# Branch prefetch hints and the order of first loads in a four-layer graph network on one core

## The chip, the cores and the metric

The kernel runs on one core of a Trainium2 chip. The metric is device time in microseconds (us); lower is better. The engines are TensorE (PE, with its weight loads as PEld), VectorE (DVE), ScalarE (ACT), GpSimd (POOL) and SyncE (SP), which only issues DMA transfers. An engine's sequencer is written with a q (DVEq): it takes instructions in order, waits on semaphores, branches and issues transfers.

## The reference

Four graph layers run one after another on 4096 nodes with 256 features, each followed by a residual sum and a layer norm. Only layers 0 and 2 meet the change.

```python
# layer 0: attention over all nodes, 8 heads of 32 channels
node_feats = (x @ W.T + b).reshape(4096, 8, 32)
logits = leaky_relu(parent[:, None, :] + child[None, :, :], 0.2)
logits = where(abs(adj) != 0, logits, 0)
out = einsum('ijh,jhc->ihc', softmax(logits, axis=1), node_feats)
...
# layer 2: two steps of diffusion R @ Xf and of top-p attention A @ Xa
for n in range(2):
    A = top_p_attention(Xa, W1, W2, W3)
    Xf, Xa = R @ Xf, A @ Xa
    Z = Z + Xf @ U1[n].T + Xa @ U2[n].T
```

## The kernel before

**Layer 0** has two stages. In the first (`sums0`, L421) the adjacency is read once. PE forms, for every node, sums over its neighbours (L601); DVE turns them into the tensor `zd` in DRAM, 33 numbers per node and head (32 channels and a count; L568 to L574). The same pass writes the adjacency as bytes (`nad`) and factored features (`gmd`) to DRAM. The engines' order in this loop is written out by hand (`manual_schedule`), over slots n of four column blocks each.

A flag `fits` says whether the factored way is safe for these numbers. If it is 0, `choose0` (L375) runs `general0`, a slow general way. For these inputs the flag is 1: every engine loads it (TENSOR_LOAD), takes the branch over `general0` (COMPARE_BRANCH) and goes on behind it. At the join each engine brings its semaphores to the value that the skipped code would have left (EVENT_SEMAPHORE on L375); SP does so for the semaphores of the transfers, which includes a wait for the last stores of `zd`.

In the second stage (L298 to L370) there are two halves of four heads; each half goes over four blocks `it` of 1024 rows, and each block over its four heads `hh`. One head is 8 groups g of four column blocks, and per group 32 matmuls (L331, 256 per head) of a mask `gt` with `gm`, the factored features. ACT or DVE compare the row logits `lpb` (a broadcast row of 512 KB) with column logits (`sg`, L270 and L276), and DVE ands the result with the bytes `na` (L272, L278) to form `gt`, of which there are four buffers. When a head's matmuls are done, DVE reduces `acc` (L337), scales it, adds the head's part of `zd` (tile `z`, L345) and divides.

The first head of all has its first two groups prepared in the first stage (`gt0`, `gm0`, `first`), so PE can start on them at once; its loads begin with group 2 and wrap round. The order of DMA issues before the change:

- SP: per group `na` (L301, 512 KB) and the first head's `gm` (L303, 198 KB); then the other heads' `gm` (L306, 396 KB for two groups)
- POOL: per head `lpb` (L236) and `z` (L316, 1024 pieces of 132 bytes), two buffers each
- ACT and POOL: the weights of layers 1 and 2 that `add_w1` (L778) loads: w1 (256 KB) and its bias on ACT, three attention weights (144 KB) on POOL

In this stage a scheduler sets the order of each engine's instructions, and may move a load ahead of others when it is ready: `add_w1` stands at the end of the layer in the code, and its loads are issued at 579 to 585 us.

**Layer 2** runs two steps over 32 row blocks, again in a hand-written order (`manual_schedule`), eight sections s per block. After the last but one block a flag `row` says whether any row needs mending; `mend` (L1270) holds the code for that, and it is branched over here, once per step. The last block's products follow behind the branch: transposes (L1405, L1498), their products (L1414), and diffusion products (L1617) whose pieces SP loads (L1603).

Of the kernel before, what the change touches and what calls it, by code (L numbers as in the profile page):

```python
# [9 lines left out]
F32 = mybir.dt.float32  # L10
# [9 lines left out]
ET = mybir.EngineType  # L20
# [3 lines left out]
P = 128  # L24
# [26 lines left out]
def row_broadcast(v, n):  # L51

    return bass.AP(tensor=v.tensor, offset=v.offset, ap=[[0, P], [1, n]])


class Net:
# [159 lines left out]
    def layer0(self):  # L216
        nc, tc, NB, D, N = self.nc, self.tc, self.NB, self.D, self.N
        H, C = 8, 32
# [5 lines left out]
        with ExitStack() as ctx:  # L224
# [7 lines left out]
            fac = pool.tile([P, 4, NB, H], F32, name="fac")  # L232
            lpd = dram.tile([H, N], F32, name="lpd")

            def row_logits(t, h, it):
                nc.gpsimd.dma_start(t, bass.AP(tensor=lpd.tensor, offset=lpd.offset + h * N + it * IT, ap=[[0, P], [1, IT]]))  # L236
                return t

            first = pool.tile([P, IT], F32, name="lpb0")
# [51 lines left out]
            gm = gp.tile([P, NB, H // 2, 6 * C1], BF16, name="gm")  # L291
            na = gp.tile([P, NB, IT], U8, name="na")

            later = []
            per_head = Q // 2 // (H // 2)
            for half in range(2):
                for it in range(N // IT):
                    i0 = it * Q  # L298
                    begun = 2 if it == half == 0 else 0
                    for g in [*range(begun, NB // K), *range(begun)]:  # L300
                        nc.sync.dma_start(na[:, g * K:(g + 1) * K], nad[it, :, g * K:(g + 1) * K, :])  # L301
                        if it == 0:
                            nc.sync.dma_start(gm[:, g * K:(g + 1) * K, 0], gmd[half, :, g * K:(g + 1) * K, 0])  # L303
                    for hh in range(1, H // 2 if it == 0 else 0):
                        for g in range(0, NB // K, 2):
                            nc.sync.dma_start(gm[:, g * K:(g + 2) * K, hh], gmd[half, :, g * K:(g + 2) * K, hh])  # L306
                    if half:
                        nc.sync.dma_start(X[:, i0:i0 + Q, :], xr[:, i0:i0 + Q, :])
                        y0 = work.tile([P, Q, D // 2], F32, name="y0", bufs=1)
                        nc.sync.dma_start(y0, yd[i0:i0 + Q].rearrange("b p d -> p b d"))  # L310
                    y = work.tile([P, Q, H // 2, C], F32, name="y")
                    for hh in range(H // 2):
                        h = half * (H // 2) + hh
                        lpb = row_logits(work.tile([P, IT], F32, name="lpb"), h, it) if h or it else first
                        z = work.tile([P, Q, C1], F32, name="z")
                        nc.gpsimd.dma_start(z, zd[i0:i0 + Q, :, h].rearrange("b p c -> p b c"))  # L316
                        acc = psum.tile([P, Q, 256], F32, name="acc")
                        for g in range(NB // K):

                            head0 = g < 2 and half == it == hh == 0  # L320
                            if head0:
                                gt = gt0[:, g * K:(g + 1) * K, :]
                            else:
                                gt = work.tile([P, K, IT], FP8, name="gt", bufs=4)
                                sg = work.tile([P, K, IT], FP8, name="sg", bufs=3)
                                mask(gt, sg, na[:, g * K:(g + 1) * K, :], lpb, g, h)
                            for k in range(K):
                                jc = g * K + k
                                for q in range(Q):

                                    nc.tensor.matmul(acc[:, q, :6 * C1], gt[:, k, q * P:(q + 1) * P],  # L331
                                                     gm0[:, jc, :] if head0 else gm[:, jc, hh, :],
                                                     start=(jc == 0 and q % 2 == 0),
                                                     stop=(jc == NB - 1 and q % 2 == 1))

                        red = work.tile([P, Q, 2 * C1], F32, name="red")
                        nc.vector.tensor_reduce(red, acc[:, :, :6 * C1].rearrange("p q (s c) -> p q c s", s=3),  # L337
                                                AX.X, ALU.add)

                        red = red.rearrange("p q (s c) -> p q s c", s=2)  # L340
                        nc.vector.tensor_mul(red, red, fac[:, 0:2, i0:i0 + Q, h].rearrange("p s q -> p q s").unsqueeze(3)
                                             .to_broadcast([P, Q, 2, C1]))
                        t1 = red[:, :, 0, :]
                        nc.vector.tensor_add(t1, t1, red[:, :, 1, :])
                        nc.vector.tensor_add(t1, t1, z)  # L345
                        r = work.tile([P, Q], F32, name="r")
                        nc.vector.reciprocal(r, t1[:, :, C])
                        nc.vector.tensor_mul(y[:, :, hh, :], t1[:, :, :C], r.unsqueeze(2).to_broadcast([P, Q, C]))
                        for xs in later[:per_head]:
                            self.layernorm(work, xs, xs, nc.gpsimd, bufs=6)  # L350
                        del later[:per_head]
                    y = y.rearrange("p q h c -> p q (h c)")
                    if not half:
                        nc.gpsimd.dma_start(yd[i0:i0 + Q].rearrange("b p d -> p b d"), y)
                        continue

                    if i0 + Q == NB:
                        self.add_w1()
                    engine = nc.vector if i0 + Q == NB else nc.gpsimd
                    for q in range(0, Q, 2):  # L360
                        xs = X[:, i0 + q:i0 + q + 2, :]
                        nc.gpsimd.tensor_add(xs[:, :, :D // 2], xs[:, :, :D // 2], y0[:, q:q + 2])
                        engine.tensor_add(xs[:, :, D // 2:], xs[:, :, D // 2:], y[:, q:q + 2])
                        later.append(xs)
# [7 lines left out]

    def choose0(self, fac, zd, gmd, gm0):

        with self.tc.If(self.nc.values_load(self.fits, min_val=0, max_val=1) == 0):  # L375
            self.general0(fac, zd, gmd, gm0)

    def factors0(self, wp, work, ps, both, nlc, fac):
# [42 lines left out]
    def sums0(self, both, nlc, fac, lpd, nad, zd, gmd, then, early_mask):  # L421
# [6 lines left out]
        with ExitStack() as ctx:  # L428
# [147 lines left out]
            with tc.manual_schedule(engines={ET.PE, ET.Activation, ET.DVE, ET.Pool, ET.SP}):  # L576
# [4 lines left out]
                for b in range(0, NB, 2):  # L581
                    pz = [psz.tile([P, 2, 512], F32, name="pz") for _ in range(2)]
                    masks = early_mask(work, (b - NB + 12) // 2) if NB - 12 <= b < NB - 4 else iter(())
                    for g in range(groups):
                        n = b // 2 * groups + g
                        load(n + 2)
                        cast(n + 1)
                        if g % 4 == 0:
                            stages = factored(b + g // 4)
                        if before and g < 2:  # L590
                            closed(b - 2, g, before[g])
                        next(stages)
                        if g in (3, 5):
                            next(masks, None)
                        ar = ready.pop(n)
                        for q in range(2):
                            for k in range(G):
                                jc = g * G + k
                                for s in range(2):
                                    for t in range(2):  # L600
                                        nc.tensor.matmul(pz[q][:, t, :W], ar[:, q, k, :], src[:, jc, t, s],  # L601
                                                         start=(jc == 0 and s == 0), stop=(jc == NB - 1 and s == 1))
                    before = pz
# [173 lines left out]

    def add_w1(self):  # L778
        nc, pool = self.nc, self.pool1
        self.weight1, self.bias1 = self.load_w(pool, self.w1, "w1"), self.load_row(pool, self.b1, "bias1")  # L780
        aw1, aw3, aw2, _ = self.attention_parts()
        for t, w in ((aw1, self.aw1t), (aw3, self.aw3t)):
            nc.gpsimd.dma_start(t, w.rearrange("(c p) m -> p c m", p=P))
        nc.gpsimd.dma_start(aw2, self.aw2t)

    def attention_parts(self):

# [78 lines left out]
    def layer2(self):  # L866
# [3 lines left out]
        with ExitStack() as ctx:  # L870
# [395 lines left out]
            def mend(step, row, flag, e, r, made=()):  # L1266


                spare = es[(NB - 2) % 3][:, :N]
                with tc.If(flag == 0):  # L1270
                    for i in range(N // 512):
                        nc.sync.dma_start(kT[:, i * 512:(i + 1) * 512].bitcast(F32), kd[i])
                    with tc.For_i(0, NB - 1, 1) as b:
# [372 lines left out]
            for step in range(2):  # L1646
# [62 lines left out]
                with tc.manual_schedule(engines=five):  # L1709
                    for b in range(NB - 1):  # L1710
# [14 lines left out]
                        for s in range(8):  # L1725
# [63 lines left out]
                                nc.sync.dma_start(kd[b - 2], kT[:, cols].bitcast(F32))  # L1789
                            if s == 0 and difs:  # L1790
                                whole(difs)
                            if s == 4 and not ahead:
                                row = settled()
                                next(row)
# [260 lines left out]
```

## Time and profile before

| what | us |
|---|---|
| median of 3 runs (3929.32 to 3931.58) | 3931.0 |
| the profiled execution | 3932.46 |
| its span | 3930.8 |
| PE idle in the span, 3930.8 - 3872.5 | 58.3 |
| last matmul of L601 ends | 572.76 |
| first matmul of L331 | 578.14 |
| the 65th matmul of L331 (group 2) | 589.51 |
| the 257th matmul of L331 (head 1) | 608.68 |
| join of the first `mend`: PE idle | 2593.36 to 2595.03 |
| join of the second `mend`: PE idle | 3673.21 to 3673.97 |

Times in the span count from its start. A row of instructions reads: line, engine, operation, what it writes and reads, how often; then busy time and mean duration; then the idle time of the engine just before, and what ended it. A row of waits reads: the engine and the line that waited, what it waited for, the total in us, how often, the longest. A row of the windows gives start and end, then busy time and (count) for each engine, the clock granted to PE, the busy share of the 16 DMA engines, and GB/s. A row of a line's sequencer gives the count, shortest/median/longest in ns, and when the first and the last began.

### The profile page before, as it was taken

To read this page: it belongs to the slowest core of one execution; us is meant where nothing else is said; L and a number is where in the kernel's file an instruction comes from. 1 tells how busy PE (TensorE), PEld (TensorE's weight loads), DVE (VectorE), ACT (ScalarE), POOL (GpSimd) and SP (SyncE) were. 2 spreads that over 40 slices of the span, in tenths; PEclk is the share of its full clock that TensorE was granted. 3 is DMA by queue.
4 is the path that set the end of the run, shared out by engine and by line. 5 is a ranking of instruction groups with operands and counts; after the bars stand their busy time and mean duration, and the time that the engine had idled before them with its cause. 6 is when DMAs were issued, how large, how long until landed. Compare 5 with 4: busy or idle time off the path is not lost. (4 is left out here: it accounts for less than half of the span.)

```text
span 3930.8 us, 68793 instructions
## 1 busy us (share of the span) xinstructions
PE 3872.5 (99%) x25081; PEld 3360.1 (85%) x25081; DVE 2995.1 (76%) x6637; ACT 2742.3 (70%) x5121; POOL 1162.8 (30%) x1402
## 2 busy tenths in 40 slices
PE   8999999999999999999999999999999999999998
PEld 7999989999999887578888888876888888888786
DVE  6444449999999544768787878848999999999464
ACT  4443449999999322568888888836888888888232
POOL 1222220111444222411111111114566555555211
PEclk9999999999999999999999999999999999999999
DMA  4666657334221696533333232463333333336541
GB/s 119 201 206 205 219 187 214 93 108 129 73 82 60 247 384 266 151 114 109 105 101 100 95 103 93 138 220 109 109 112 114 112 115 101 107 108 205 208 149 45
DMA packets 319870, 561.58 MB, mean 143 GB/s; under 512 B 73063, under 2 KB 140151, under 8 KB 315415
## 3 DMA queue, kind: packets, MB, share of 16 engines
q1 hardware_dynamic: 244832, 401.18, 31.4%
q0 software_dynamic: 32224, 98.75, 7.8%
q10 hardware_dynamic: 42454, 57.04, 4.2%
q8 instruction: 203, 3.33, 0.3%
q14 instruction: 157, 1.28, 0.1%
HBM read 386.71 MB, written 170.13 MB: 142 GB/s over the span
## 5 line engine op out<-in xcount | busy, mean ns | idle before, releaser
L1414 PE MATMUL ps_a<-X,aT 128*128 128x256 f32 x4096 | 969.1, 379 | 1.6 <-ACT h L1558 1.1
L1414 PEld LDWEIGHTS ps_a<-X,aT 128*128 128x128 f32 x4096 | 773.2, 190 | 127.4 <-issue 3.3
L331 PE MATMUL acc<-gm,gt 128*128 128x198 bf16 x8192 | 702.9, 248 | 12.4 <-DVEq L375 5.4
L331 PEld LDWEIGHTS <-gt 128*128 128x128 fp8e4 x8192 | 700.8, 97 | 14.5 <-issue 9.7
L276 ACT ACTIVATE sg<-lpb,nlc 128x1024 fp8e4<-128x1024 f32 x632 | 664.1, 1135 | 45.4 <-DVE gt L278 32.5
L180 PE MATMUL ps_r<-XD,adj_piece 128*128 128x512 f32 x1888 | 528.4, 414 | 0.0
L601 PE MATMUL pz<-src,ar 128*128 128x264 f32 x4096 | 500.6, 285 | 0.4 <-DVE big L399 0.4
L601 PEld LDWEIGHTS pz<-src,ar 128*128 128x128 f32 x4096 | 500.4, 189 | 0.5 <-issue 0.5
L1139 ACT ACTIVATE ja<-e,nc 128x2048 uint8<-128x2048 f32 x240 | 480.9, 2004 | 2.0
L1407 ACT COPY aT<-ps_tp 128x512 f32<-128x512 f32 x512 | 295.9, 578 | 207.6 <-PE ps_tp L1405 201.6
L180 PEld LDWEIGHTS ps_r<-XD,adj_piece 128*128 128x128 f32 x1888 | 333.0, 189 | 68.8 <-issue 12.9
L1204 DVE MAX8 cand<-v 128x8 f32<-128x256 f32 x1024 | 347.1, 411 | 4.4
L1254 DVE SCALAR_TENSOR_TENSOR e<-e,edge 128x512 f32<-128x512 f32 x512 | 346.8, 749 | 2.1
L561 ACT ACTIVATE nb<-ar 128x512 uint8<-128x512 f32 x256 | 147.6, 623 | 280.0 <-DVE ar L558 164.6
L1405 PE MATMUL ps_tp<-ident,e 128*128 128x128 f32 x2048 | 307.3, 273 | 2.4 <-DVEq L1270 1.7
L1200 DVE SCALAR_TENSOR_TENSOR v<-e,hi 128x2048 f32<-128x2048 f32 x128 | 301.4, 2355 | 2.4
L1405 PEld LDWEIGHTS ps_tp<-ident,e 128*128 128x128 f32 x2048 | 255.9, 141 | 54.1 <-issue 2.6
L558 DVE CAST ar<-a 128x1024 fp32r<-128x1024 f32 x128 | 88.9, 694 | 267.3 <-PE pz L601 267.2
L270 DVE TENSOR_SCALAR sg<-lpb,nlc 128x1024 fp8e4<-128x1024 f32 x384 | 285.3, 778 | 6.7 <-SPq L375 4.6
L1048 ACT ACTIVATE e<-ps_logit 128x1024 f32<-128x1024 f32 x256 | 259.9, 1025 | 27.1 <-PE ps_logit L1046 26.8
L1046 PE MATMUL ps_logit<-kT,q 128*128 128x512 f32 x1024 | 273.9, 409 | 1.5 <-ACT e L1048 0.9
L854 PE MATMUL ps_adj<-XD,adj_piece 128*128 128x512 f32 x1024 | 239.8, 394 | 0.0
(408 smaller groups left out, 5587.4 us busy)
## 6 DMA issues: line engine op xcount, KB each, us to landing
adj_piece<-adjs SPq DMA_DIRECT2D x504, 256.0 KB, 2.8
a<-in_adjt_dram SPq DMA_DIRECT2D x256, 256.0 KB, 3.0
adjs<-adj_piece SPq DMA_DIRECT2D x96, 512.0 KB, 3.3
na<-nad SPq DMA_DIRECT2D x64, 512.0 KB, 5.4
lpb<-lpd POOLq DMA_DIRECT2D x32, 512.0 KB, 4.4
nad<-nb POOLq DMA_DIRECT2D x128, 128.0 KB, 2.7
na<-nad ACTq DMA_DIRECT2D x16, 1024.0 KB, 8.8
gmd<-gb POOLq DMA_DIRECT2D x64, 198.0 KB, 2.7
```

The lines of the kernel that those rows point to most:

```text
L180: nc.tensor.matmul(ps, a[:, k, :], rhs(jc).rearrange("p s d -> p (s d)"), start=(jc == 0), stop=(jc == self.NB - 1))
L270: nc.vector.tensor_scalar(sg[:, k, :], lpb, nlc[:, 4 * g + k, h:h + 1], 2.0 ** -5, op0=ALU.is_ge, op1=ALU.mult, saturate=False)
L276: nc.scalar.activation(sg[:, k, :], lpb, AF.Sign, scale=-1.0, bias=nlc[:, 4 * g + k, h:h + 1], saturate=False)
L331: nc.tensor.matmul(acc[:, q, :6 * C1], gt[:, k, q * P:(q + 1) * P], gm0[:, jc, :] if head0 else gm[:, jc, hh, :], start=(jc == 0 and q % 2 ...
L601: nc.tensor.matmul(pz[q][:, t, :W], ar[:, q, k, :], src[:, jc, t, s], start=(jc == 0 and s == 0), stop=(jc == NB - 1 and s == 1))
L1139: nc.scalar.activation(ja, e[:, s * HALF:(s + 1) * HALF], f, bias=nc1, accum_out=fs[:, i + s:i + s + 1])
L1200: nc.vector.scalar_tensor_tensor(v, ec, hi, ec, op0=ALU.is_lt, op1=ALU.mult, accum_out=sb[:, s:s + 1])
L1204: nc.vector.max(cand[:, 8 * j:8 * j + 8], v[:, k * 256:(k + 1) * 256])
L1254: nc.vector.scalar_tensor_tensor(ec, ec, edge[:, j:j + 1], ec, op0=ALU.is_ge, op1=ALU.mult)
L1405: nc.tensor.transpose(pt[:, k * P:(k + 1) * P], e[:, jc * P:(jc + 1) * P], self.ident)
L1407: nc.scalar.copy(aT, pt)
L1414: nc.tensor.matmul(pa[:, :D], aT[:, k * P:(k + 1) * P], X[:, jc, :], start=(jc == 0), stop=(jc == NB - 1))
```

## The change

1. The branches round `general0` and the two `mend` get labels. Ahead of each, a hint instruction that names the label is put on PE, DVE, SP and ACT: in layer 0 in the last slot of the first stage, in layer 2 in the last section of the last block before the branch. POOL gets none.
2. `z` is loaded once per half and block for four heads (1024 pieces of 528 bytes) into a tile with one buffer, instead of once per head. For the very first block that load and head 1's `lpb` are issued on SP behind group 4's loads; elsewhere `z` stays on POOL.
3. The loads of `add_w1` go to SP instead of ACT and POOL.

```diff
+            def products_of(i0, half, queue):
+                z = work.tile([P, Q, H // 2, C1], F32, name="z", bufs=1)
+                queue.dma_start(z, zd[i0:i0 + Q, :, half * H // 2:(half + 1) * H // 2].rearrange("b p h c -> p b h c"))
+                return z
...
                         if it == 0:
                             nc.sync.dma_start(gm[:, g * K:(g + 1) * K, 0], gmd[half, :, g * K:(g + 1) * K, 0])
+                        if begun and g == 4:
+                            z = products_of(i0, half, nc.sync)
+                            second = row_logits(work.tile([P, IT], F32, name="lpb"), 1, 0, nc.sync)
+                    if not begun:
+                        z = products_of(i0, half, nc.gpsimd)
...
-                        lpb = row_logits(work.tile([P, IT], F32, name="lpb"), h, it) if h or it else first
-                        z = work.tile([P, Q, C1], F32, name="z")
-                        nc.gpsimd.dma_start(z, zd[i0:i0 + Q, :, h].rearrange("b p c -> p b c"))
+                        lpb = (first, second)[h] if it == 0 and h < 2 else \
+                            row_logits(work.tile([P, IT], F32, name="lpb"), h, it)
...
-                        nc.vector.tensor_add(t1, t1, z)
+                        nc.vector.tensor_add(t1, t1, z[:, :, hh, :])
...
-        with self.tc.If(self.nc.values_load(self.fits, min_val=0, max_val=1) == 0):
+        with self.tc.If(self.nc.values_load(self.fits, min_val=0, max_val=1) == 0, label="general0"):
...
+                        if n == slots - 1:
+                            tc.mark_branch_hint_location("general0", engines=[ET.PE, ET.DVE, ET.SP, ET.Activation])
...
-        self.weight1, self.bias1 = self.load_w(pool, self.w1, "w1"), self.load_row(pool, self.b1, "bias1")
+        self.weight1 = pool.tile([P, 2, self.D], F32, name="w1")
+        nc.sync.dma_start(self.weight1, self.w1.rearrange("(c p) m -> p c m", p=P))
+        self.bias1 = pool.tile([P, self.D], F32, name="bias1")
+        nc.sync.dma_start(self.bias1, row_broadcast(self.b1, self.D))
...
-            nc.gpsimd.dma_start(t, w.rearrange("(c p) m -> p c m", p=P))
-        nc.gpsimd.dma_start(aw2, self.aw2t)
+            nc.sync.dma_start(t, w.rearrange("(c p) m -> p c m", p=P))
+        nc.sync.dma_start(aw2, self.aw2t)
...
-                with tc.If(flag == 0):
+                with tc.If(flag == 0, label=f"mend{step}"):
...
+                            if s == 7 and not ahead:
+                                tc.mark_branch_hint_location(f"mend{step}", engines=[ET.PE, ET.DVE, ET.SP, ET.Activation])
```

## The prediction

> **What bounds the kernel now.** I read the page first, for the busiest engine; then TensorE's waits, to see where it stands; then the lines of the two branches, and the windows round the first.
>
> ```profile
> PE 3872.5 (99%) x25081; PEld 3360.1 (85%) x25081; DVE 2995.1 (76%) x6637; ACT 2742.3 (70%) x5121; POOL 1162.8 (30%) x1402
> ...
> L331 PE MATMUL acc<-gm,gt 128*128 128x198 bf16 x8192 | 702.9, 248 | 12.4 <-DVEq L375 5.4
> ```
>
> TensorE (PE) is busy for 99% of the span: 3930.8 - 3872.5 = 58.3 us idle in all. An edit that takes no matmul away can gain only there, or where the matmuls run slowly. TensorE's waits place it:
>
> ```profile
> PE acc L331 <- DVEq L375: 5.4, 1, 5.4
> PE acc L331 <- DMA gm<-gmd: 4.0, 1, 4.0
> ...
> PE ps_tp L1405 <- DVEq L1270: 1.7, 1, 1.7
> ...
> PE ps_tp L1498 <- PEq L1270: 0.8, 1, 0.8
> ```
>
> Four waits belong to the change: both branches of layer 2 (L1270) with 1.7 and 0.8, the branch round layer 0's general way (L375) with 5.4, and 4.0 behind it for the first `gm` load. At L375:
>
> ```profile
> L375 PEldq COMPARE_BRANCH  x1: 3694/3694/3694, 571.2 to 571.2; - x1
> ...
> L375 DVEq COMPARE_BRANCH  x1: 72/72/72, 575.1 to 575.1; - x1
> L375 SPq COMPARE_BRANCH  x1: 53/53/53, 575.1 to 575.1; - x1
> L375 DVEq EVENT_SEMAPHORE  x1: 21/21/21, 578.0 to 578.0; - x1
> ```
>
> DVE and SP branch at 575.1 and do their next thing at 578.0: 2.9 us with nothing to wait for. At L1270 PE's branch takes 359 ns once and 3888 ns once, and ACT's next event comes 0.13 us after its branch. So a taken branch costs either 0.1 to 0.4 us or 2.8 to 3.9 us; in the long ones 16,384-byte packets of the instruction queues run. I read that as code being fetched.
>
> The windows show what idling costs besides:
>
> ```profile
> 568.12:574.95 6.83, 4.64 (x39) 4.42 (x37) 3.65 (x11) 0.63 (x1) 1.10 (x2) 1.00 0.32 104
> 574.95:581.78 6.83, 3.64 (x23) 3.35 (x24) 2.53 (x4) 2.18 (x3) 2.04 (x3) 0.50 0.29 88
> 581.78:588.60 6.82, 3.72 (x43) 3.58 (x42) 3.15 (x4) 6.25 (x7) 3.50 (x5) 1.00 1.02 296
> 588.60:595.43 6.83, 5.92 (x37) 5.39 (x37) 3.85 (x5) 2.62 (x3) 0.00 (x0) 0.50 1.08 339
> 595.43:602.26 6.83, 6.83 (x83) 6.83 (x81) 6.79 (x9) 6.05 (x7) 0.00 (x0) 1.00 1.09 360
> ```
>
> The column before the last two is the granted clock: 0.50 in two stretches, each just after an idle piece. A matmul there starts 165 ns after the one before, elsewhere 85. The last two columns show the DMA engines saturated (share 1.02 to 1.09) from 581.8 on.
>
> **Part 1: the hint at layer 0.** Removed: the fetch behind the branch on DVE, SP, PE and ACT. DVE ends its last sum at 574.7 and branches until 575.13; with ACT's 0.13 us it frees PE at about 575.4 instead of 578.14 (PE's own branch begins at 571.2, so it is long done). PE starts 2.7 us earlier. POOL gets no hint; its branch ends at 570.4 and its next work is 7 us later, which hides it.
>
> SP has one more wait: its second join event waits for the last `zd` store, issued at 574.7. Fifteen of that store's sixteen parts land by 576.45, the sixteenth at 578.63; a 16 KB instruction packet of 1.75 us runs meanwhile. With the fetch done earlier I take 576.5, so SP's first `na` load moves from 579.45 to 577.3: -2.2 us. If the straggler stays, it moves nothing; that bound is kept for the range.
>
> **Part 2: the loads.** What head 1 (256 matmuls after the first) needs ends with the first `gm` piece of its own (L306). It lands at 607.1, and head 1 starts at 608.7. Since the DMA engines are saturated, I price every load ahead of it by the time of its packets on 16 engines. Gone from that stretch: w1 on ACT's queue, 256 x 55 ns / 16 = 0.9 us; the attention weights on POOL's, 144 KB at some 320 KB/us = 0.5; two `z` loads of 132-byte pieces, 64 packets x 430 ns / 16 = 1.7. Added: one `z` for four heads, 1024 pieces of 528 bytes. No such packet is in the trace; between the 396-byte one (25 ns, 1.6 us in all) and the 1024-byte one (55 ns, 3.5 us) I take 33 ns, 2.1 us, being nearer the first in size. `lpb` for head 1 only changes queue (issue on SP instead of POOL: the same bytes), and SP, whose issues are held up by full queues (3.57 us for one `na` at 584.2), issues two loads more; that time is the transfers' own and already counted. So the piece lands at 607.1 - 2.2 - 3.1 + 2.1 = 603.9.
>
> Is PE ready by then? It starts at 575.4. At half clock to 581.78 it does 38 of the first 64 matmuls, then 26 x 85 ns: 584.0. (Before: 585.3.) The next group's `na` and `gm` are then first in SP's queue with only one `lpb` beside them; counting 1.2 MB at 340 KB/us from 578.8 gives 583, so the 4.0 us wait goes. Six groups of 32 x 85 ns = 2.72 us follow: 600.3 without stalls. The group behind the moved `z` and `lpb` (g = 5) lands at about 592.7 and costs a us or so. So head 0 is done by 601.5 and what comes last is the transfer: head 1 starts at about 604.0 instead of 608.7, **-4.7 us**. DVE and ACT (98% and 96% busy from 620 to 1120) make masks 3 to 4 us earlier too, against a lead of 4 us over PE now; I cost that at nothing, and at 1 to 2 us if the lead is used up.
>
> After head 1 starts, its pieces come every 1.7 us and PE takes 5.4 us for one: no new stall. The 24 fewer `z` loads (0.9 us each on POOL) lie beside matmuls. The single `z` buffer is freed by head 3's sum, 6 us into the next head, and is wanted 16 us later; a load lands in 3.3 us. w1 and the rest, on SP now, are wanted at 1290, and SP has hundreds of us: nothing.
>
> **Part 3: the hints at layer 2.** First branch: PE resumes at 2595.03 because DVE's event came at 2594.87, 3.1 us after its branch; its own work was done at 2592.6. PE's last matmul ends at 2593.36, so PE could go on at 2593.8: 1.2 us earlier. But at 2598.96 it takes a `kT` piece that landed at 2598.63, from an SP issue that waits for PE's own end and does not move. So 0.3 stays; range 0.2 to 1.3. Second branch: PE's 3.89 us ended at 3673.5, its queue of matmuls at 3673.21: 0.3.
>
> The twelve hint instructions are in no row. An instruction more cannot gain; nearest are 0.02 to 0.05 us for an event and 0.18 us for a register operation, on sequencers that run ahead of their engines: nothing, at most 0.5 us on PE.
>
> **Sum.** 4.7 + 0.3 + 0.3 = 5.3 us. The profiled execution took 3932.5 (span 3930.8 and 1.7 round it), 1.5 above the median of 3931.0. So 3927.2 for it, and **3925.7** for the median.
>
> **Rivals.**
> (a) *The hints start no fetch.* Then 578.14 and 579.45 stay, and only the loads differ: the piece lands at 607.1 - 1.0 = 606.1, head 1 gains 2.5: 3928.5. For it: nothing in this trace shows a branch target fetched ahead. Against: the 359 ns branch shows that code present costs little. [...] Chance 0.16.
> (b) *The transfers keep up* (better order, fewer small pieces). Then PE sets head 1: 600.3, a gain of 8.4, with layer 2 about 9.2: 3921.8. If the 2.7 us idle leaves the clock full, the first 64 end at 580.9 and all ends 3.1 earlier: 3918.7. Against: share 1.0 and more for 20 us. [...] Chance 0.20.
> (c) *Slower: `z` blocks POOL.* If an iteration's `z` stands ahead of its first head's `lpb` on POOL, that `lpb` waits for head 3's sum: 6 us after the head's last matmul, plus 0.9 and 0.6 of issue, 4.1 to land and 5.8 for the first mask: 17 us of idle PE, seven times, 120 us: 4045. It decides as soon as this order is emitted. Against: POOL's queue now runs by readiness (the L783 loads, from the end of the layer, at 583.3, ahead of the third `z`), and that `lpb` is ready some 30 us before its `z`. Chance 0.05.
>
> **How the numbers follow.** The forecast has 0.52, (a) 0.16, (b) 0.20, (c) 0.05; 0.07 is left for slips of 1 to 3 us either way. A change under 0.2%, 7.9 us, is about what a measurement of this kernel cannot tell from none. Only (b) passes that: faster 0.23. The forecast and (a) lie within: 0.70. Slower 0.07. The range takes in (a), most of (b), and a straggler that stays: 3920 to 3931.5.
>
> **What would show it.** Right: DVE's event at L375 0.1 to 0.4 us after its branch; PE's wait there about 2.7 us and the `gm` wait gone; head 1's first matmul 31 us after layer 0's last sum matmul instead of 36; a short wait for `gm` before it. Wrong: events still 2.8 us behind branches (a), no wait before head 1 (b), PE waits of 10 us and more every four heads (c).

## The result, and the profile after

The changed kernel took **3921.89 us** (median of 12 runs, 3919.38 to 3929.10); the kernel before, run beside it, 3931.26 (12 runs). The medians lie 9.4 us apart. The ratio is 0.9979, with a 95% interval of 0.9971 to 0.9986: faster by 8.3 us, or 5.5 to 11.4. The forecast was 3925.7. It has the sign right, and 4 us too little.

The profiled execution took 3925.49 us (span 3923.8). Four phases, each measured at TensorE's (PE's) matmuls, compare it with the profile before: the first stage to its last matmul; layer 0's heads, to the start of the last of their matmuls; the rest, to PE's last matmul; and the tail to the end of the span.

| us | before | after | difference |
|---|---|---|---|
| first stage | 572.76 | 574.07 | +1.3 |
| heads of layer 0 | 715.00 | 709.29 | -5.7 |
| rest (end of layer 0, layers 1 to 3) | 2629.52 | 2631.34 | +1.8 |
| tail after PE's last matmul | 13.48 | 9.08 | -4.4 |
| span | 3930.8 | 3923.8 | -7.0 |

The first stage and the rest contain the clock's chance. The first stage had 10.2 us at half clock instead of 6.8, the rest 10.2 instead of 6.8; 3.4 us at half clock (granted 0.50) cost 1.7. The gain sits in the heads and in the tail.

**The join of layer 0.** PE's waits, from the answer that lists what each engine waited for (total us, times, longest us):

```profile
PE acc L340 <- DVEq L384: 3.0, 1, 3.0
PE acc L340 <- DMA gm<-gmd: 2.6, 2, 1.7
...
PE acc L340 <- DVE gt L272: 1.5, 1, 1.5
...
PE ps_tp L1419 <- PEq L1284: 0.5, 1, 0.5
...
PE ps_tp L1512 <- PEq L1284: 0.4, 1, 0.4
```

L340 is L331 of before, L384 is L375, and L1284 is L1270. The wait at the join fell from 5.4 to 3.0, the single 4.0 for `gm` became two short ones (1.7 at group 2, 1.0 before head 1), and the two `mend` joins cost 0.5 and 0.4. The branch's own rows on the sequencers (count, shortest/median/longest ns, first and last start):

```profile
L384 PEldq COMPARE_BRANCH  x1: 399/399/399, 572.6 to 572.6; - x1
...
L384 DVEq COMPARE_BRANCH  x1: 84/84/84, 576.4 to 576.4; - x1
L384 SPq COMPARE_BRANCH  x1: 73/73/73, 576.4 to 576.4; - x1
L384 DVEq EVENT_SEMAPHORE  x1: 21/21/21, 577.0 to 577.0; - x1
```

PE's branch takes 399 ns instead of 3694, and DVE's event follows the end of its branch by 0.5 us instead of 2.9. The kernel with the hints alone (e_hints below) shows the same: 391 ns and 0.5 us. So the hints do make the branches cheap; I read that as a fetch of the target that starts ahead of the branch, which no row shows by itself.

The windows behind the join, at the same times as before (busy time and count of PE, PEld, DVE, ACT and POOL; then PE's granted clock, the DMA share and GB/s):

```profile
568.12:574.95 6.83, 5.95 (x49) 5.73 (x48) 3.31 (x9) 1.29 (x3) 1.85 (x3) 1.00 0.26 84
574.95:581.78 6.83, 4.67 (x38) 4.42 (x39) 3.75 (x7) 3.45 (x4) 0.54 (x1) 0.75 0.43 130
581.78:588.60 6.82, 5.15 (x61) 4.95 (x59) 4.58 (x6) 5.00 (x6) 0.00 (x0) 1.00 1.03 303
588.60:595.43 6.83, 5.62 (x67) 5.38 (x64) 5.59 (x7) 4.25 (x4) 0.00 (x0) 1.00 1.12 359
595.43:602.26 6.83, 6.57 (x78) 6.57 (x79) 4.92 (x7) 6.59 (x7) 0.00 (x0) 1.00 1.09 348
```

Only half a window runs at half clock, against two whole ones before; the idle piece in which it begins is 3.0 us long, those before were 5.4 and 4.0. The DMA engines are still saturated from 581.8 on (share 1.03 to 1.12). Head 1 starts 30.92 us after the first stage's last matmul instead of 35.92, behind a last wait of 0.97 for `gm`: the transfers still come last.

**The tail.** The last line's rows on the sequencers of POOL and SP, before and then after:

```profile
L2051 POOLq DRAIN  x3: 44/113/9528, 3920.4 to 3930.5; - x3
L2051 SPq DRAIN  x3: 7/7/13, 3923.6 to 3930.2; - x3
```

```profile
L2067 POOLq DRAIN  x3: 40/113/5117, 3917.8 to 3923.5; - x3
L2067 SPq DRAIN  x3: 7/7/13, 3920.7 to 3923.2; - x3
```

When POOL's last work is done it drains, and the last events of ACT, DVE and PE (3930.1 and 3930.7; after the change 3923.1 and 3923.7) come behind that. The drain took 9.528 us before, from 3920.4 to 3929.9, while SP had been done with the last store since 3923.7. After the change it took 5.117, to 3922.9, and SP was done at 3920.7. The prediction priced neither this row nor its change.

The same view shows where the hints are carried out:

```profile
L2067 ACTq BRANCH_PREFETCH_HINT  x3: 38/47/50, 0.8 to 2588.1; - x3
L2067 SPq BRANCH_PREFETCH_HINT  x3: 31/46/56, 0.8 to 2588.8; - x3
L2067 DVEq BRANCH_PREFETCH_HINT  x3: 39/50/51, 0.8 to 2588.5; - x3
L2067 PEldq BRANCH_PREFETCH_HINT  x3: 36/36/50, 0.9 to 2589.4; - x3
```

They do not run where the source marks them. Each stands at the start of a stretch of code: `general0`'s 0.8 us into the program, the first `mend`'s right behind the join at L384, the second's behind the first `mend`. Each takes 31 to 56 ns.

### The profile page after: what moved, and what is told of

It is laid out like the page before. It is cut to its first block, busy times and chain, and to the rows that moved or that the text cites. A ratio compares the mean times of both kernels' runs of the same rounds, so it can differ in the third digit from the quotient of the medians.

```text
span 3923.8 us, 68735 instructions
## 1 busy us (share of the span) xinstructions
PE 3872.9 (99%) x25081; PEld 3359.6 (86%) x25081; DVE 2997.0 (76%) x6637; ACT 2741.5 (70%) x5121; POOL 1138.2 (29%) x1373
## 3 DMA queue, kind: packets, MB, share of 16 engines
q1 hardware_dynamic: 247056, 402.79, 31.6%
## 5 line engine op out<-in xcount | busy, mean ns | idle before, releaser
L340 PE MATMUL acc<-gm,gt 128*128 128x198 bf16 x8192 | 699.8, 248 | 9.8 <-DVEq L384 3.0
L340 PEld LDWEIGHTS <-gt 128*128 128x128 fp8e4 x8192 | 698.2, 97 | 11.3 <-issue 6.0
```

## The experiments

Twelve kernels. "Before" and "after" are the two kernels of this case. The columns are: PE's wait at the layer 0 join; start of head 1 after the first stage; the heads; the rest; PE's wait for ACT near 2618; POOL's drain (all from one profile each); the median; and the ratio to the kernel before, run on the same chip.

| kernel | join | head 1 | heads | rest | ACT stall | drain | median us | ratio (95%) |
|---|---|---|---|---|---|---|---|---|
| before | 5.38 | 35.9 | 715.0 | 2629.5 | none | 9.53 | 3931.3 | |
| after | 3.05 | 30.9 | 709.3 | 2631.3 | none | 5.12 | 3921.9 | 0.9979 (0.9971 to 0.9986) |
| e_hints | 3.05 | 34.1 | 713.2 | 2635.5 | 3.6 | 9.53 | 3935.2 | 1.0010 (1.0001 to 1.0018) |
| e_loads | 5.31 | 33.7 | 711.9 | 2631.8 | none | 5.12 | 3926.9 | 0.9988 (0.9980 to 0.9997) |
| e_zloads | 5.37 | 34.9 | 713.9 | 2632.8 | none | 5.94 | 3931.4 | 0.9998 (0.9989 to 1.0007) |
| e_weights | 5.64 | 33.3 | 712.4 | 2630.6 | none | 7.73 | 3930.2 | 1.0001 (0.9992 to 1.0010) |
| e_hints_noact | 3.04 | 32.4 | 711.5 | 2627.6 | none | 9.53 | 3929.4 | 0.9995 (0.9986 to 1.0004) |
| e_after_noact | 3.11 | 30.9 | 709.2 | 2626.9 | none | 5.12 | 3923.3 | 0.9981 (0.9972 to 0.9990) |
| e_drain1 | 3.04 | 31.6 | 711.6 | 2628.7 | none | 5.93 | 3925.2 | 0.9985 (0.9975 to 0.9995) |
| e_drain128 | 3.19 | 32.1 | 710.5 | 2631.1 | none | 6.67 | 3927.2 | 0.9985 (0.9975 to 0.9995) |
| e_hints_act | 5.33 | 35.4 | 714.5 | 2638.6 | 4.1 | 9.53 | 3939.4 | 1.0018 (1.0009 to 1.0027) |
| e_hints_actpart | 3.04 | 31.9 | 711.0 | 2637.6 | 3.7 | 9.53 | 3934.3 | 1.0006 (0.9997 to 1.0015) |
| e_w1back | 3.04 | 32.2 | 710.4 | 2632.8 | 3.9 | 5.94 | 3930.7 | 0.9998 (0.9989 to 1.0007) |
| e_zlate | 3.05 | 29.5 | 707.7 | 2626.1 | none | 5.12 | 3920.9 | 0.9974 (0.9963 to 0.9985) |

A profile is one execution, and "rest" moves by 1.7 us with each 3.4 us that happens to run at half clock. The columns at the join, head 1, stall and drain are steadier: the drain is the same to 0.01 us in kernels with the same POOL transfers.

### The hints alone, the loads alone

e_hints is the kernel before with all three hints on all four engines, as in this diff; e_loads is the changed kernel with the same lines taken back.

```diff
-        with self.tc.If(self.nc.values_load(self.fits, min_val=0, max_val=1) == 0):
+        with self.tc.If(self.nc.values_load(self.fits, min_val=0, max_val=1) == 0, label="general0"):
...
+                        if n == slots - 1:
+                            tc.mark_branch_hint_location("general0", engines=[ET.PE, ET.DVE, ET.SP, ET.Activation])
...
-                with tc.If(flag == 0):
+                with tc.If(flag == 0, label=f"mend{step}"):
...
+                            if s == 7 and not ahead:
+                                tc.mark_branch_hint_location(f"mend{step}", engines=[ET.PE, ET.DVE, ET.SP, ET.Activation])
```

> The kernel before with the three hints alone. If the ledger of the two profiles is right: DVE's join event at L375's branch about 0.5 us after it instead of 2.9, SP's first na load about 2 us earlier against the end of the first stage, head 1 starts about 34 us after the first stage's last matmul instead of 35.9 (the transfers still come last), the two waits behind the mend branches go to about 0.5 us each, -1.0 to -1.4 together. Sum: 3 to 3.5 us faster. POOL's DRAIN at the end: its queue is untouched, so 9 to 10 us as before if POOL's queue sets it; anywhere between 5 and 10 us if it is chance. Rival (a), hints fetch nothing: no change.

> The change without its hints (the loads of the heads and of the weights alone). The join stays as before (DVE's event 2.9 us after the branch, PE idle 5.4 us); head 1 starts 33 to 34 us after the first stage's last matmul (the prediction's rival (a): a gain of 2.5 us); no gain at layer 2. If POOL's queue sets the DRAIN at the end, it takes about 5 us here instead of 9.5, another 4.4 us: 6 to 7 us faster in all. If the DRAIN is chance: 2 to 3 us faster.

The loads alone gave 5 us: 3.2 in the heads and 4.4 in the drain, with some 2 given back in the rest, where the first `mend` join cost 2.3 instead of 1.7 and PE waited 1.2 us longer for DVE near 2724. Without hints the join stays at 5.3.

The hints alone **lost** 3 us, though each join went at least as well as forecast and head 1 started at +34.1. PE has a wait here, in layer 2, that neither kernel of the case has:

```profile
PE acc L331 <- DMA gm<-gmd: 6.0, 1, 6.0
...
PE ps_tp L973 <- ACT X L969: 3.6, 1, 3.6
PE acc L331 <- DVEq L375: 3.1, 1, 3.1
```

The second row is new. (The first shows that 2.0 of the 2.3 us won at the join were waited off again for `gm`.) What held ACT there is the matter of the third group.

### The two load edits apart

e_zloads is the kernel before with the `z` tile for four heads, and the first `z` and head 1's `lpb` on SP; e_weights is the kernel before with the five loads of `add_w1` on SP. The edits are those of the change's diff, of which these are the first lines of each:

```diff
+            def products_of(i0, half, queue):
+                z = work.tile([P, Q, H // 2, C1], F32, name="z", bufs=1)
...
-        self.weight1, self.bias1 = self.load_w(pool, self.w1, "w1"), self.load_row(pool, self.b1, "bias1")
+        self.weight1 = pool.tile([P, 2, self.D], F32, name="w1")
+        nc.sync.dma_start(self.weight1, self.w1.rearrange("(c p) m -> p c m", p=P))
...
```

> The kernel before with z for four heads and the first block's z and second lpb on SP; the weights stay on ACT and POOL, no hints. POOL issues 26 transfers fewer than before. If POOL's transfers set the DRAIN: about 5.5 us, and 5 to 6 us faster in all; head 1 starts about 34.5 us after the first stage's last matmul (the weights' 1.4 us come back). If the DRAIN is chance: 1 to 2 us faster.

> The kernel before with add_w1's five loads on SP alone; z and lpb as before, no hints. POOL issues 3 transfers fewer. If the DRAIN goes with the number of POOL's transfers, it stays at 9 us or more; the first gm piece of head 1 lands about 1.4 us earlier, so head 1 starts 34.5 us after the first stage's last matmul: about 1.4 us faster, hardly to be told from none. If the DRAIN is chance, anything between 5 and 10 us.

In the profiles both help: head 1 starts 1.0 and 2.6 us earlier, and the drain is 3.6 and 1.8 us shorter. The medians show nothing that can be told from no change. In e_zloads the rest took 3.3 us longer, with the same time at half clock; in e_weights it took 1.1 longer with 3.4 us less of it. 1.2 us of it is one wait: PE waits 1.9 us for DVE near 2728 (near 2722 in e_weights), against 0.7 at the same place before, and 30 us ahead of that DVE's operation `v<-e,hi` takes 4.12 us instead of 2.35. Both are in all nine kernels with either load edit and in none of the five without, so the load edits bring them; how is not shown. The rest, some 2 us, stays open. That e_weights' drain shrank to 7.73 also goes against its expectation of 9 us or more: three transfers of 515 made 1.8 us. The weights' part of the start of head 1 is more than the transfers priced in the prediction for it (0.9 + 0.5 us).

### ACT's stall

Five kernels. e_hints_noact (on the kernel before) and e_after_noact (on the changed one) hint PE, DVE and SP alone. e_hints_act is the kernel before with hints on ACT alone. e_hints_actpart is e_hints, except that ACT gets no hint for the second `mend`. e_w1back is the changed kernel with `add_w1` as before: w1 on ACT's queue, three loads on POOL's. The edits of the first four, as lists of engines:

```diff
-engines=[ET.PE, ET.DVE, ET.SP, ET.Activation]
+engines=[ET.PE, ET.DVE, ET.SP]
...
-engines=[ET.PE, ET.DVE, ET.SP, ET.Activation]
+engines=[ET.Activation]
...
-                                tc.mark_branch_hint_location(f"mend{step}", engines=[ET.PE, ET.DVE, ET.SP, ET.Activation])
+                                tc.mark_branch_hint_location(f"mend{step}", engines=[ET.PE, ET.DVE, ET.SP] + ([] if step else [ET.Activation]))
```

> The kernel before with the three hints on PE, DVE and SP, but none on ACT. Theory 1: the hints on ACT cost ACT a fetch of its own straight code later on (in the kernel with all hints ACT stood still for 3.67 us at 2618 with nothing to wait for, and PE with it for 3.56 us, then at half clock for 6.83 us). Then without ACT's hints this stall is gone, the wait at the first join stays at 3.05 us (ACT branches 4 us before DVE, so its own fetch is hidden), head 1 starts at +34, and the time is 3.0 to 3.5 us below before, about 3928. Rival 1: the stall comes from where the code lies, not from ACT's hints: then a stall of 3 to 4 us stays on some engine and the time is 3932 to 3936. Rival 2: ACT's late event now frees PE at the first join: its wait is 5 us again and the time is that of before.

> The changed kernel without the hints on ACT. Theory 1 (ACT's hints cost a later fetch, and only where the code lies badly): its profile of the changed kernel shows no ACT stall of that kind, so the time is that of the changed kernel, 3921 to 3923, with PE's wait at the first join at 3.05 us and POOL's last drain at 5.117 us. Rival 1 (position alone): a new stall of 3 to 4 us may come up on an engine, since the code lies otherwise: 3925 to 3928. Rival 2 (ACT then frees PE at the join): 3.05 becomes about 5.4 and head 1 starts at +33 instead of +30.9: 3924 to 3925.

> The kernel before with the three hints on ACT alone. Theory 1 (ACT's hints make ACT fetch straight code late): ACT stands still for 3 to 4 us near 2618 with no releaser, PE with it, and PE runs at half clock for 3.4 to 6.8 us after it. The first join keeps its wait of 5.4 us, so nothing is won: the time is 5 to 7 us above before, 3936 to 3939. Rival (where the code lies, with hints on all engines): no stall, the time is that of before, 3930 to 3933.

> The kernel before with all hints but one: ACT is not told of the second branch of layer 2, the hint that ACT carries out at 2588, some 30 us before its stall at 2618. Theory 1a (this hint is what disturbs ACT's fetching): no stall, 3928 to 3930 as without any hint on ACT. Rival 1b (an earlier hint, or the place of the code): the stall of 3.6 us is there, 3934 to 3936.

> The changed kernel with the loads of layer 1's weights back on ACT and POOL. ACT's stream is then, up to layer 2, that of the kernel before with all hints, which stalled, while the changed kernel, shorter by one load on ACT, did not. If a hint stalls ACT only where the code lies badly, the stall of 3.6 us at 2618 comes back with half clock behind it: 3928 to 3930. If the place is nothing, no stall: 3922 to 3924. In both POOL's last drain is 5.93 us, as in the kernel before with only the sums' loads changed, which has the same transfers on POOL: 0.8 us of the time above. Head 1 starts at +32 in both, as w1 is again among the transfers.

Without hints on ACT the stall is gone and the join's gain stays (e_hints_noact, e_after_noact); the 2.4 us by which e_hints_noact's median lies below the kernel before are inside its interval. With hints on ACT alone nothing is won at the join and the stall is there. PE's waits in e_hints_act:

```profile
PE acc L331 <- DVEq L375: 5.3, 1, 5.3
...
PE acc L331 <- DMA gm<-gmd: 4.1, 1, 4.1
PE ps_tp L973 <- ACT X L969: 4.1, 1, 4.1
```

ACT's instructions between 2600 and 2625, in e_w1back and then in the changed kernel (busy and mean ns; then idle time before them and what ended it):

```profile
L978 ACT COPY X<-ps_logit 128x1024 f32<-128x1024 f32 x4 | 4.1, 1013 | 6.4 <-issue 4.0 <-PE ps_logit L977 2.3
```

```profile
L981 ACT COPY X<-ps_logit 128x1024 f32<-128x1024 f32 x5 | 5.1, 1015 | 1.8 <-PE ps_logit L980 1.7
```

"issue" means that ACT waited for nothing that the profile shows, and here that is 4.0 us. The records of the instruction queues name it: in each of the four kernels with the stall an 8,192-byte packet starts 1.57 us before ACT goes on.

| kernel | packet starts | ACT goes on |
|---|---|---|
| e_hints | 2619.10 | 2620.67 |
| e_hints_act | 2620.03 | 2621.60 |
| e_hints_actpart | 2616.60 | 2618.17 |
| e_w1back | 2613.99 | 2615.57 |

ACT runs straight code here, some 30 us behind its branch round the first `mend`; I read this as its next code coming too late, by the times of the packets alone. In these four kernels PE waits 3.6 to 4.1 us for it, in the others not at all.

The stall costs twice. In e_w1back the windows around it show PE at half clock right behind:

```profile
2607.80:2614.70 6.90, 4.86 (x27) 3.40 (x25) 1.80 (x3) 1.65 (x3) 0.00 (x0) 1.00 0.85 266
2614.70:2621.50 6.80, 4.86 (x8) 2.50 (x8) 0.68 (x1) 1.34 (x2) 0.00 (x0) 0.50 0.10 38
2621.50:2628.40 6.90, 6.90 (x40) 4.81 (x39) 2.83 (x5) 3.30 (x6) 0.00 (x0) 1.00 0.68 182
```

3.9 us of waiting and 6.8 us at half clock make 7.3 us lost. All four show that 6.8 us stretch.

Two expectations fell. That the hint for the second `mend`, carried out 30 us ahead of the stall, is its cause: without it (e_hints_actpart) the stall is there. That a hint on ACT is enough: the changed kernel has all three and no stall. What held is that the place decides: e_w1back was expected at 3928 to 3930 with the stall, stalls, and took 3930.7. **Moving `add_w1`'s loads to SP, which the prediction priced through their transfers at 1.4 us, is worth 8.8 us between the medians of the changed kernel and e_w1back** (3921.9 against 3930.7; 7.5 by the ratios 0.9979 and 0.9998, whose intervals do not touch). An estimate from the rows comes near: 7.3 for the stall, which goes with the two loads on ACT, 0.8 for the drain, which goes with the three on POOL, and 1.1 in the heads make 9.2. The spans of the two profiles do not show it: they differ by 1.2 us, as e_w1back's execution was the fastest of its kernel (3926.69) and had 6.8 us less at half clock in all than the changed kernel's, which was one of its slower ones (3925.49).

What sorts the kernels is where the code lies. Counted in the traces, the third X copy of layer 2 (L967 of before) is ACT's instruction number

| 3626 to 3629, no stall | 3631, 3632, stall |
|---|---|
| before 3629, after 3629, e_drain1 and e_drain128 3629, e_hints_noact 3629, e_zloads 3628, e_weights 3627, e_loads, e_after_noact and e_zlate 3626 | e_hints_actpart and e_w1back 3631, e_hints and e_hints_act 3632 |

Before (no hint) and after (three hints) stand at the same number, because the change takes two loads and one event off ACT and adds three hints. So the number sorts all fourteen profiles. But the late code is not in the four kernels alone. The instruction that starts late in them is number 3631 each time. In the three kernels with hints on ACT and no stall, number 3631 also starts 1.6 us behind such a packet:

| kernel | packet starts | number 3631 starts | after number 3630 |
|---|---|---|---|
| after | 2616.17 | 2617.78 | 0.59 |
| e_drain1 | 2616.15 | 2617.74 | 0.30 |
| e_drain128 | 2615.69 | 2617.28 | 0.03 |

There the X copy that PE waits for, number 3629, is already done, and ACT waits 2.8 us for DVE before number 3630 in any case. I read that as hiding the late code; PE is busy for 6.71 of the 6.80 us from 2612.80 on in the changed kernel. In the four with the stall the copy is number 3631 itself or stands right behind it. The seven kernels without hints on ACT do not show a late number 3631: in before and e_hints_noact it starts 1.18 and 1.40 us behind a packet and less than 0.01 us after number 3630, and in the other five no packet of this size starts between 1 and 20 us before it. So two things go with the stall: a packet that starts 1.57 to 1.61 us ahead of number 3631, which all seven kernels with hints on ACT have, and a copy that stands at that number or behind it, as e_w1back against the changed kernel shows with the same hints. Whether it is the hints that make the code late, or only the other layout of ACT's stream, stays open: no kernel whose stream was lengthened without hints was run.

### POOL's drain

Both kernels are the changed one with sixteen more loads on POOL in `add_w1`, of one piece each in e_drain1 (below) and of 128 pieces each in e_drain128 (`more[:128, k]` from `self.w1[:128, ...]`). Nobody reads them.

```diff
+        more = pool.tile([P, 16, 4], F32, name="more")
+        for k in range(16):
+            nc.gpsimd.dma_start(more[:1, k], self.w1[:1, 4 * k:4 * k + 4])
```

> The changed kernel with 16 more POOL loads of one piece (16 bytes) each, whose tile nobody reads, issued where the weights of layer 1 are loaded. POOL's last drain took 9.53 us with 515 loads and stores on POOL (before), 7.73 with 512 (weights on SP), 5.94 with 489 (sums loaded four heads at once), 5.12 with 486 (both). Theory count: the drain goes with the number of POOL's transfers: at 0.27 us for each (the difference of the last two) it takes 9.5 us here. Theory pieces: it goes with the number of pieces in the transfers, and 16 more pieces are nothing: 5.12 us. Theory of a wrap: it goes with a count modulo some size, and may rise or fall by some us.

> As the kernel with 16 more POOL loads, but of 128 pieces each (2048 pieces in all). Theory count: the same drain as that kernel, 9.5 us. Theory pieces: the weights' loads put back (576 pieces or so) made 0.82 to 1.80 us, so 2048 pieces make the drain 3 to 6 us longer, 8 to 11 us, while the other kernel stays at 5.12. Theory of a wrap: another value than both.

The rows of the drain in e_drain1 and in e_drain128:

```profile
L2070 POOLq DRAIN  x3: 46/113/5928, 3916.4 to 3922.9; - x3
```

```profile
L2070 POOLq DRAIN  x3: 40/112/6668, 3919.0 to 3926.3; - x3
```

With nothing else changed on POOL, the drain rose from 5.12 to 5.93 and 6.67. So it does depend on what POOL's queue has issued in the whole program, 3300 us earlier. But neither theory with a number holds: by the count of transfers both should be 9.5, by pieces the first should be 5.12 and the second 8 to 11. The third, a count that wraps, gave no number that these two could refute. And the three weight loads on POOL, which move together with w1's two on ACT in e_w1back and e_weights, take it from 5.12 to 5.94 on the changed kernel, but from 7.73 to 9.53 on the one before. The law stays open; that the change's fewer POOL transfers shortened it by 4.4 us is measured, not explained.

### A later place for the first z

The transfers still set head 1's start, so the load that is wanted last was put behind a piece that is wanted first, on top of e_after_noact:

```diff
                         if begun and g == 4:
-                            z = products_of(i0, half, nc.sync)
                             second = row_logits(work.tile([P, IT], F32, name="lpb"), 1, 0, nc.sync)
...
                             nc.sync.dma_start(gm[:, g * K:(g + 2) * K, hh], gmd[half, :, g * K:(g + 2) * K, hh])
+                            if begun and hh == 1 and g == 2:
+                                z = products_of(i0, half, nc.sync)
```

> The changed kernel without ACT's hints, and with the very first load of the sums moved behind the second piece of head 1's gm. It takes about 2 us of transfers out of the way of what head 1 waits for. Theory (the transfers come last): head 1 starts at +29 instead of +30.9, and the time is 1 to 2 us below the changed kernel, 3920 to 3922. Rival (DVE takes their place): head 0's sum on DVE waits for the sums' load, the masks behind it come late, and PE waits 1 to 3 us more within head 1: 3922 to 3924.

Head 1 started at +29.5 instead of +30.9, and PE's only waits between 570 and 640 were these:

```profile
PE acc L341 <- DVEq L385: 3.0, 1, 3.0
PE acc L341 <- DMA gm<-gmd: 2.9, 1, 2.9
```

The waits at `z` and before head 1 are gone, and DVE did not take their place. 3920.9 us is the lowest median here, 1.0 us below the changed kernel; that difference is inside both intervals, so only the 1.4 us in the profiles is shown.

## Why the prediction was right, and where it was not

- **The join (2.7 us earlier): right in mechanism.** PE started 2.33 us sooner after the first stage's end. DVE's event comes 0.5 us after its branch, not 0.13: a branch with a hint is not quite as cheap as the row of ACT suggested. The prediction's 2.8 to 3.9 us for a dear branch also leaves out ACT's own at L375, whose event followed by 2.4. SP's first `na` load moved by 2.05 (forecast 2.2).
- **Part 2, head 1 31.2 us after the first stage: right.** Measured 30.9, with the wait for `gm` before it that the forecast wanted and rival (b) did not; the stall for g = 5 was 1.5 instead of "a us or so". Two steps on the way were off: the wait for `gm` at group 2, of which the prediction says that it goes, stayed with 1.7 of its 4.0 us, and the first 1.2 MB at 340 KB/us from 578.8 give 582.4, not 583. The 528-byte packet, which had no row, took 34.8 ns on the mean, 2.2 us in all, against 33 and 2.1. The rest of the heads gained 0.7 more.
- **Rival (b) gave 3921.8, the time that came, by luck** (and by its own terms 8.4 + 0.3 + 0.3 make 9.0, so 3922.0). Its mechanism did not come: head 1 would have started at 27.5. Only e_zlate goes a step that way.
- **Rival (a) is refuted** by 3694 ns against 399 ns, and e_loads shows that the hints are worth 2 to 3 us at this join.
- **Rival (c) did not occur:** no wait of 10 us recurs.
- **Part 3: mis-sized for the first branch.** 1.1 us instead of 0.3. The last `kT` piece, which was to land late, landed 4.2 us after PE's last matmul instead of 5.3. The second branch gave 0.3, as forecast.
- **The step that failed: "The 24 fewer z loads (0.9 us each on POOL) lie beside matmuls" and "w1 and the rest, on SP now [...]: nothing".** They do lie beside matmuls, but POOL's last drain reflects them, and it ends the span: -4.4 us. This is what the forecast lacks. In the profiles the heads' -5.7, the tail's -4.4 and the two `mend` joins' -1.4 make -11.5; layers 1 to 3 otherwise gave 3.2 back (1.7 at half clock near 3710, 1.2 in a longer wait for DVE near 2722, behind an operation at 2691 that took 4.1 us instead of 2.4), and the first stage 1.3. The medians show 9.4. Without the drain that would be some 5 us, near the forecast's 5.3; that it is so near is partly luck, since the heads and the joins won 7.1 and other places gave some back.
- **"Nothing, at most 0.5 us on PE" for the hint instructions was right for this kernel and for no good reason.** The same hints with their stall cost 7 us where ACT's stream is two instructions longer. The prediction looked at the cost of the instructions and at the engine that bounds; it did not ask where a longer stream puts ACT's instructions against the code that comes late, nor did it see that the loads taken off ACT's queue make up for it.

## What to carry to other kernels

Read the last link too: what ends the span here is POOL's drain, 6.2 us after SP was done with the last store before the change and 2.2 after it, and edits to POOL's transfers moved it though they lay fully hidden. Put a prefetch hint only on engines whose late branch someone waits for: ACT branched 6.1 us ahead of DVE, and without a hint its next event still came 4 us before DVE's (e_hints_noact), so its hint could win nothing; without it nothing was lost that the medians can tell (3923.3 against 3921.9). And when an edit that should be neutral costs 3 to 8 us, look for idle time that ends with "issue" and an instruction-queue packet: here two or three instructions more on ACT, a far-off engine, put the copy that PE waits for at or behind the place where, as I read it, the code comes late, and PE waited 3.6 to 4.1 us.

## What the hardware showed unexpectedly

- A hint works from far off. `general0`'s was carried out at 0.8 us and its branch came at 576.4; the second `mend`'s at 2588, with the branch at 3665.7. Both branches were cheap: DVE's at the join took 84 ns, with its event 0.5 us behind it (2.9 before), and PE's at the second `mend` 346 ns (3888 before).
- In the two profiles of this case half clock came, up to PE's last matmul, in stretches of 3.41, 6.83 or 10.24 us. In the four kernels with the stall, 6.83 us of it went with the PE wait of 3.56 to 4.05 us in layer 2 each time. In layer 0 such stretches began within PE's waits of 5.4 and 4.0 us (before, 6.83 us each, at 574.95 and 588.60) and of 3.0 us (after, 3.41 us, at 576.83), and one followed a wait of 2.9 us (e_zlate, at 584.6).
- POOL's final drain was the same in all kernels with the same POOL transfers (9.527 to 9.528 us in five kernels, 5.117 to 5.120 in four) and differed by up to 4.4 us between kernels with others.
